# Stacking x1 on the hop-0 sums in a two-layer graph network: one product for x1 and its hop-1 share, own shares moved into the first row

## The chip, the core and the metric

The kernel runs on one core of a Trainium2 chip. The metric is device time in microseconds for one execution. The engines are called by short names: PE is TensorE (matmuls; PEld are its weight loads), DVE is VectorE, ACT is ScalarE, POOL is GpSimd, and SP issues the DMAs (SPq is its queue).

## What is computed

Two layers of a graph network over 4096 nodes with 64 features. The adjacency matrix `adj` is 4096 x 4096 fp32 and mostly zero. Layer 0 makes two hops, each with a sum over neighbours, a product with a weight matrix of 128 x 64 and a tanh. Layer 1 keeps, for each node, its last 100 neighbours at most, each weighted by a power of one half that depends on its rank in the row.

```python
# layer 0
h = maximum(layernorm(x), 0)
for k in range(2):
    agg = adj @ h
    h = tanh(concatenate([agg, h], axis=1) @ W[k])
x = x + h
# layer 1
h = maximum(layernorm(x), 0)
support = h @ weight
mask = (adj != 0)
rank = cumsum(mask, axis=1); deg = rank[:, -1:]
k = minimum(deg, 100); pos = rank - (deg - k)
w = mask * where(pos > 0, 0.5 ** (k - pos), 0)
x = x + (w @ support + bias)
```

## The kernel before

The nodes are cut into 4 chunks of 1024 (`NCH`, called `I`, or "rows" of the first sweep), each of 8 blocks of 128. Everything is fp32 but the layer-1 weights.

**Sweep 1** (lines 403 to 493) reads the whole matrix once, in 64 pairs of blocks `k` (16 pairs a row, so row 0 is pairs 0 to 15). `load` (line 411) issues the loads some pairs ahead, into a ring of three pair slots and into the areas that later hold the codes. For each pair two things happen. `count_pair` (line 232) marks the non-zero elements (on DVE at line 238, or before that on ACT by `mark_on_act`, lines 229 and 230, which for row 0 is written two pairs ahead) and counts them into codes, for layer 1. And TensorE adds `adj @ h` to the row's sums: at line 256 with 64 stationary columns into `acc_low` (two column halves `c` of the array side by side), or at line 468 ("fused") with 128 stationary columns, h0 and, for chunks whose x1 is already known, x1 as well, so that hop 1 is begun in the same pass. `features_T` (line 273, after pairs 4, 6, 9 and 13) transposes a chunk's h0 on TensorE into one of the two single-buffer PSUM banks `one` and `two` and ACT copies it into `pre1`, where it waits as the "own" operand.

At a row's end `finish_row` (line 338) is put on the list `steps`, of which each later pair runs one step. Step 1 copies the sums out of PSUM on ACT (`T` for h0's sums, `Fx` for x1's sums) and makes the row's totals (`totals`, line 286: an add on DVE, a cast on ACT). Step 2 is `x1_of` (line 213): two products, one with T and one with the own operand in `pre1`, into bank `po`, and a tanh on ACT (line 217) to `x1T`. Step 3 is `x1_and_share` (line 310): products of the transposed `Fx` with a weight (line 319) and of the transposed `x1T` with `both_w`, which is the identity beside the hop-1 weight (line 324). So the banks hold x1 by nodes and its share of hop 1; `take` (line 334) copies them out on ACT. Step 4 is `set_after` (line 291). In row 0 a further step adds the own-chunk sums.

**Sweep 2** (from line 764) reads the blocks of `adj` that hop 1 still lacks, 512 KB at a time, through the ring, and runs layer 1 at the same time. `finish_last` (line 503) finishes row 3 in steps, as `finish_row` does for the others. `finish_x2` (line 536) ends hop 1 of a chunk: S is copied from PSUM (line 541, ACT), four products `py` (line 551), add, tanh, residual, layernorm, and the features of layer 1. The order of all work is written out ahead by a planner in Python: `clock` holds a planned time for each engine, `use(engine, us, after)` moves it, and `decode`, `convert` (lines 637 to 663: code to weight, on ACT at 661 or DVE at 653 and 656), `settle` (line 396) and `layer1` (line 703) choose by these clocks what is written next. So a changed `use` can change the order.

The weights come in by one DMA, `load_weights` (line 147), issued before pair 9; POOL then spreads them (lines 151 and 154). POOL also has the `pow` of every layernorm (line 195).

Of the kernel before, what the change touches and what calls it, by code (L numbers as in the profile page):

```python
# [8 lines left out]
F32 = mybir.dt.float32  # L9
# [10 lines left out]
P = 128  # L20
# [23 lines left out]
def gnn_kernel(  # L44
# [73 lines left out]
    def tmp(shape=None, dtype=F32, name="tmp"):  # L118
        return tpool.tile(shape or [P, C], dtype, tag="tmp", name=name)
# [27 lines left out]
    def load_weights():  # L147
        nc.sync.dma_start(wb, weights)
        for h in range(2):
            rows = slice(h * D, (h + 1) * D)  # L150
            nc.gpsimd.tensor_copy(
                wz[rows, h], wb[rows, : HOPS * 2].rearrange("p (k a) e -> p k a e", a=2)
            )
        nc.gpsimd.tensor_copy(both_w[:, 1, :].rearrange("p (h e) -> p h e", h=2), wz[:, :, 1, 1, :])

    warm = spool.tile([P, 1], F32, tag="warm", name="warm")
    nc.vector.memset(warm, 0.0)
# [8 lines left out]
    both_w = cpool.tile([P, 2, P], F32, name="both_w")  # L166
    ident = both_w[:, 0, :]
    nc.vector.tensor_scalar(ident, diff, 0.0, None, op0=ALU.is_equal)

    tri = cpool.tile([P, P], BF16, name="tri")  # L170
    nc.vector.tensor_scalar(tri, diff, 0.0, -1.0, op0=ALU.is_lt, op1=ALU.mult)
# [32 lines left out]
    def paired(po, terms):  # L204

        for n, (w, v) in enumerate(terms):
            for c in range(NC):
                nc.tensor.matmul(  # L208
                    po[c * D : (c + 1) * D, :], w(c), v(c),
                    start=n == 0, stop=n == len(terms) - 1,  # L210
                )

    def x1_of(po, I, terms):

        paired(po, terms + [(lambda c: wz[:, c, 0, 1], lambda c: flat(pre1[:, chunk(I), :]))])
        x1T = tmp(name="x1T")
        nc.scalar.activation(x1T, po, AF.Tanh)
        return x1T

    as_nodes = lambda ap: ap.rearrange("p (c t) e -> p t c e", c=NC)  # L220

# [64 lines left out]
    def totals(I, both, tot):  # L286

        nc.vector.tensor_tensor(both.bitcast(U16), cnts[I % 2][0], cnts[I % 2][1], op=ALU.add)  # L288
        nc.scalar.copy(tot, both)  # L289
# [17 lines left out]
        )  # L307
        nc.vector.tensor_scalar(early, early, float(K), None, op0=ALU.min)

    def x1_and_share(I, x1T, Fx):  # L310

        banks = [one(name="pt"), two(name="pt")]
        v = by_t(x1T)
        for h, pt in enumerate(banks):
            pt = pt.rearrange("p (t w q) -> p t w q", t=2, w=2)
            if Fx is not None:
                f = by_t(Fx)
                for t in range(2):
                    nc.tensor.matmul(  # L319
                        pt[:, t, 1, :].rearrange("p (c e) -> p c e", c=NC), f[:, h, t, :], wz[:, :, 1, 0, :],  # L320
                        start=t == 0, stop=False, skip_group_check=True,
                    )
# [15 lines left out]
    def finish_row(I, acc, held):  # L338
        if I:

            T = [tmp(name="T") for _ in range(NC)]
            for c in range(NC):
                nc.scalar.copy(T[c][:D], acc[0][:D, c, :])
                nc.scalar.copy(T[c][D:], acc[1][c * D : (c + 1) * D])
# [4 lines left out]
        else:  # L349
            S = tmp(name="S")  # L350
            nc.scalar.copy(S, acc[1])
            Fx = None
# [50 lines left out]
    def sweep1():  # L403
# [28 lines left out]
        for k, (I, b) in enumerate(pairs):  # L432
# [3 lines left out]
            if k == 0:  # L436
# [66 lines left out]
    def finish_last(acc):  # L503

        I = NCH - 1
        bytes_ = mbuf.rearrange("p a r i -> p (a r i)")
        tot = bytes_[:, 2 * CW :].bitcast(BF16)
        totals(I, bytes_[:, :CW], tot)
        S = tmp(name="S")
        nc.scalar.copy(S, acc[1])  # L510
        F = [tmp(name="F") for _ in range(NC)]
        for c in range(NC):
            nc.scalar.copy(F[c], acc[0][:, c, :])
        Fx = tmp(name="Fx")
# [4 lines left out]
        po = one(name="po")  # L519
        x1T = x1_of(  # L520
            po, I, [(lambda c: wz[:, c, 0, 0], lambda c: S), (lambda c: wz[:, 0, 0, 0], lambda c: F[c])]
        )
        use("ACT", 0.65, use("PE", 2.3) + 0.2)
        yield
        banks = x1_and_share(I, x1T, Fx)
        take(hxs[I][:, :, D:], banks, 0)
        take(pre1[:, chunk(I), :], banks, 1)
        use("ACT", 1.5, use("PE", 2.8) + 0.2)
        yield
        set_after(I, tot, [one(name="pb"), two(name="pb")])  # L530
        feats[2] = place([P, CB, 2 * D], F32R, "cnt", "feat")
        use("DVE", 2.9, use("PE", 0.5) + 0.2)
        all_settle(I)
        space(feats[2].rearrange("p b d -> p (b d)"), clock["DVE"], 2)

    def finish_x2(I, acc):
# [1 line left out]

        h = chunk(I)
        S = tmp(name="S")  # L540
        nc.scalar.copy(S, acc)
        xres = tmp([P, CB, D], name="xres")
        nc.sync.dma_start(xres, x[I])
        state["gap"] = 1.35, 2.2
        t = use("ACT", 0.6, clock["PE"] + 0.2) + 0.1
        yield t

        pt = one(name="py")
# [364 lines left out]
```

## Time and profile before

| | |
|---|---|
| median of 3 runs | 368.76 us (367.73 to 369.48) |
| profiled execution, its own time | 367.51 us |
| its span in the profile | 365.7 us |
| PE busy | 340.6 us, 93% |
| DVE busy | 284.2 us, 78% |
| ACT busy | 205.3 us, 56% |
| POOL busy | 24.1 us, 7% |
| chain that ended last | PE 73%, DMA 15%, ACT 5%, SPq 4%, issue 2% |

The lines of the chain, by line of code, begin with PE L468 (23%), PE L256 into `acc` (16%), PE L703 (15%), PE L256 into `acc_low` (10%); the products that the change touches are L208 (3%), L319 (1%) and L324 (2%). The weights' DMA took 17.2 us from issue to landing.

How to read it: a row of a timeline has start, length, engine, line, operation, output and inputs, shape and count, and in brackets how long the engine stood idle before it and for whom. A matmul in fp32 has two records. The span leaves out some 1.8 us that the device time includes.

### The profile page before, as it was taken

The numbers are of one execution on the slowest core, as the hardware profiler recorded it, in microseconds if no ns is written. First come the engines' busy times: TensorE is split into PE (matmuls) and PEld (weight loads), VectorE is DVE, ScalarE is ACT, GpSimd is POOL, SyncE is SP. The second block draws the span as 40 slices with busy tenths as digits, with TensorE's granted clock in tenths as the row PEclk, the third lists the DMA queues.
The fourth block names the chain that finished last, engine by engine and source line by source line (L and its number), as shares of the span: only waits on it lengthen the run. The fifth ranks groups of instructions, "written<-read, shape, count | busy, mean of one in ns | idle before, by whom it ended". The sixth has DMA issues, their size and how long they took to land.

```text
span 365.7 us, 3966 instructions
## 1 busy us (share of the span) xinstructions
PE 340.6 (93%) x1356; PEld 151.9 (42%) x1356; DVE 284.2 (78%) x514; ACT 205.3 (56%) x230; POOL 24.1 (7%) x21
## 2 busy tenths in 40 slices
PE   3887789999999999999999998979999999989996
PEld 0242124333453444444444432333444444447585
DVE  4998989489998999979998965946587615858993
ACT  2286982576069260550000522777879699639991
POOL 2221100000000000000000002103100110003000
PEclk9999999999999999999999999999999999999998
DMA  7999999999994979639889989949888889830002
GB/s 289 414 409 407 408 409 409 409 411 407 409 398 185 356 283 392 237 117 359 324 299 340 314 270 411 323 169 323 311 286 284 318 293 318 328 126 0 2 30 86
DMA packets 29827, 108.45 MB, mean 297 GB/s; under 512 B 2416, under 2 KB 2800, under 8 KB 29808
## 3 DMA queue, kind: packets, MB, share of 16 engines
q1 hardware_dynamic: 29808, 108.21, 79.2%
q8 instruction: 10, 0.16, 0.2%
q14 instruction: 9, 0.07, 0.1%
HBM read 107.15 MB, written 1.05 MB: 296 GB/s over the span
## 4 chain that ended last, share of the span: by engine, by line
PE 73%; DMA 15%; ACT 5%; SPq 4%; issue 2%; DVE 0%; ACTq 0%
PE acc L468 23%; PE acc L256 16%; PE accl L703 15%; PE acc_low L256 10%; DMA codes<-in_adjA_dram 9%; DMA ring<-in_adjA_dram 6%; SPq L428 3%; PE po L208 3%; PE pto L754 2%; PE pt L324 2%; ACT weights L661 2%; PE py L551 1%; ACT codes L229 1%; PE pt L319 1%; ACT codes L230 1%
## 5 line engine op out<-in xcount | busy, mean ns | idle before, releaser
L661 ACT ACTIVATE weights<-codes,zero 128x1024 fp32r<-128x1024 uint8 x96 | 101.6, 1136 | 13.7 <-PE accl L703 10.4
L256 PE MATMUL acc<-ring,hx 128*64 128x512 f32 x288 | 70.9, 607 | 3.8 <-DMA ring<-in_adjA_dram 3.8
L703 PE MATMUL accl<-weights,feat 128*128 128x512 f32 x250 | 67.4, 409 | 0.7 <-ACT weights L661 0.6
L468 PE MATMUL acc<-ring,hx 128*128 128x512 f32 x152 | 66.1, 594 | 0.0
L256 PE MATMUL acc_low<-codes,hx 128*64 128x512 f32 x224 | 53.4, 599 | 6.4 <-DMA codes<-in_adjA_dram 6.4
L703 PEld LDWEIGHTS accl<-weights,feat 128*128 128x128 f32 x250 | 43.9, 188 | 31.0 <-ACT weights L661 15.0
L468 PEld LDWEIGHTS acc<-ring,hx 128*128 128x128 f32 x152 | 28.6, 190 | 37.1 <-issue 36.5
L250 DVE TENSOR_SCALAR cnt<-codes 128x512 uint16<-128x512 uint16 x128 | 37.7, 294 | 4.4
L249 DVE TENSOR_TENSOR codes<-mbuf,cnt 128x512 uint16<-128x512 uint16 x90 | 38.4, 426 | 3.1
L396 DVE TENSOR_TENSOR codes<-codes,after 128x2048 uint16<-128x2048 uint16 x32 | 37.7, 1218 | 0.0
L256 PEld LDWEIGHTS acc<-ring,hx 128*64 128x64 f32 x288 | 16.9, 135 | 43.9 <-issue 23.1
L256 PE MATMUL acc_low<-ring,hx 128*64 128x512 f32 x96 | 27.4, 692 | 7.7 <-DVE hx L198 6.3
L230 ACT ACTIVATE codes<-codes 128x1024 uint8<-128x1024 int8 x32 | 33.8, 1057 | 1.0
L238 DVE TENSOR_SCALAR mbuf<-ring 128x2048 uint8<-128x2048 f32 x27 | 32.9, 1220 | 0.8 <-DMA ring<-in_adjA_dram 0.8
L229 ACT ACTIVATE codes<-codes 128x1024 int8<-128x1024 f32 x24 | 25.1, 1047 | 11.7 <-DMA codes<-in_adjA_dram 11.7
L256 PEld LDWEIGHTS acc_low<-codes,hx 128*64 128x64 f32 x224 | 15.2, 136 | 37.8 <-issue 23.1
L656 DVE TENSOR_SCALAR weights<-bits 128x1024 fp32r<-128x1024 f32 x29 | 20.1, 694 | 9.9 <-PE accl L703 4.4
L238 DVE TENSOR_SCALAR mbuf<-codes 128x2048 uint8<-128x2048 f32 x21 | 25.6, 1219 | 0.0
L570 POOL TENSOR_TENSOR pre<-pre,wb 128x512 f32<-128x512 f32 x4 | 5.1, 1281 | 270.6 <-DVE xc L190 270.6
L289 ACT CAST mbuf<-mbuf 128x1024 bf16<-128x1024 uint8 x1 | 1.0, 1045 | 37.7 <-DVE mbuf L288 37.7
L653 DVE TENSOR_SCALAR bits<-codes 128x1024 uint32<-128x1024 uint8 x29 | 20.0, 690 | 0.6
L195 POOL TENSOR_TENSOR s<-s,half 128x8 f32<-128x8 f32 (+2 forms) x9 | 17.3, 1923 | 33.2 <-DVE s L194 33.2
(87 smaller groups left out, 252.3 us busy)
## 6 DMA issues: line engine op xcount, KB each, us to landing
ring<-in_adjA_dram SPq DMA_DIRECT2D x74, 512.0 KB, 4.8
codes<-in_adjA_dram SPq DMA_DIRECT2D x33, 1024.0 KB, 15.0
ring<-in_adjA_dram SPq DMA_DIRECT2D x30, 1024.0 KB, 5.6
pre<-in_x_dram SPq DMA_DIRECT2D x4, 256.0 KB, 6.9
xres<-in_x_dram SPq DMA_DIRECT2D x4, 256.0 KB, 5.8
out_dram<-o SPq DMA_DIRECT2D x3, 256.0 KB, 2.5
out_dram<-o SPq DMA_DIRECT2D x2, 128.0 KB, 2.0
wb<-in_weights_dram SPq DMA_DIRECT2D x1, 192.0 KB, 17.2
```

Source lines behind the costliest of these rows:

```text
L229: nc.scalar.activation(sign, a[:, r], AF.Sign)
L230: nc.scalar.activation(m, sign, AF.Square, scale=float((FLAG - 1 + 0.25) ** 0.5))
L238: nc.vector.tensor_scalar(m, a, 0.0, float(FLAG - 1), op0=ALU.not_equal, op1=ALU.mult)
L249: nc.vector.tensor_tensor(q, marks[r].bitcast(U16), cnt, op=ALU.add)
L250: nc.vector.tensor_scalar(cnt, q, 0x7F7F, None, op0=ALU.bitwise_and)
L256: nc.tensor.matmul(acc[c * D : (c + 1) * D, :], src, a[:, c * C : (c + 1) * C], start=first, stop=last,)
L396: nc.vector.tensor_tensor(q, q, a[:, None, :].to_broadcast([P, 4, CW // 2]), op=ALU.subtract)
L468: nc.tensor.matmul(acc[0][:, c, :], at(g), a[:, r, c * C : (c + 1) * C], start=g == CB * I - 1, stop=g == 0,)
L653: nc.vector.tensor_scalar(state["bits"], q, float(ZERO), ONE, op0=ALU.subtract, op1=ALU.mult)
L656: nc.vector.tensor_scalar(w, state["bits"].bitcast(F32), 2.0 ** (127 - LOW), None, op0=ALU.mult)
L661: nc.scalar.activation(w, q, AF.Exp, scale=LN2, bias=zero)
L703: nc.tensor.matmul(sums[g][:, c, :], feats[J][:, k, :], w[:, c * C : (c + 1) * C], start=first, stop=last,)
```

## The change

1. `load_weights` is issued before pair 6 instead of 9. `both_w` is split into `ident` and `xw`, whose rows 0 to 63 are the identity beside x1's hop-1 weight, and rows 64 to 127 zero beside the sums' hop-1 weight; POOL fills it with two copies.
2. x1 is no longer one tile with the two halves `c` above each other, but two tiles `xs[c]`: rows 0 to 63 get x1 of half c (one tanh for each), rows 64 to 127 get x1's sums (formerly `Fx`). One product of `xs[c]` with `xw` then gives x1 by nodes and the whole share. In row 0, which has no such sums, only 64 rows are used.
3. `own_share`: after pair 12 for chunk 2 and after pair 14 for chunk 1, the own product is made and copied back into `pre1`. In rows 1 and 2 `x1_of` leaves it out of the accumulation and adds it on DVE, into `T[1]`, before the tanh.
4. In `finish_row` the totals go from step 1 to step 2, behind x1.
5. `finish_last` stacks its sums as `finish_row` does (`T` from `acc` and `acc_low`), so that the three products of `x1_of` become two. Its `use` constants change.
6. In `finish_x2` the copy of S goes to ACT or DVE, whichever planned clock is behind.

```diff
-        nc.gpsimd.tensor_copy(both_w[:, 1, :].rearrange("p (h e) -> p h e", h=2), wz[:, :, 1, 1, :])
+        nc.gpsimd.tensor_copy(xw[:D, 1, :], wb[:D, 3, :])
+        nc.gpsimd.tensor_copy(xw[D:, 1, :], wb[D:, 2, :])
...
+    xw = cpool.tile([P, 2, D], F32, name="xw")
+    nc.vector.tensor_scalar(xw[:, 0, :], diff[:, :D], 0.0, None, op0=ALU.is_equal)
...
-    def x1_of(po, I, terms):
+    def x1_of(po, I, terms, xs, at_=None):
-        paired(po, terms + [(lambda c: wz[:, c, 0, 1], lambda c: flat(pre1[:, chunk(I), :]))])
-        x1T = tmp(name="x1T")
-        nc.scalar.activation(x1T, po, AF.Tanh)
-        return x1T
+        own = (lambda c: wz[:, c, 0, 1], lambda c: flat(pre1[:, chunk(I), :]))
+        paired(po, terms + [own] * (at_ is None))
+        if at_ is not None:
+            nc.vector.tensor_tensor(at_, po, flat(pre1[:, chunk(I), :]), op=ALU.add)
+            po = at_
+        for c in range(NC):
+            nc.scalar.activation(xs[c][:D], po[c * D : (c + 1) * D, :], AF.Tanh)
+
+    def own_share(I):
+        h = flat(pre1[:, chunk(I), :])
+        po = (two if I % 2 else one)(name="po")
+        paired(po, [(lambda c: wz[:, c, 0, 1], lambda c: h)])
+        nc.scalar.copy(h, po)
...
-    def x1_and_share(I, x1T, Fx):
+    def x1_and_share(I, xs):
         banks = [one(name="pt"), two(name="pt")]
-        v = by_t(x1T)
+        K_ = P if I else D
         for h, pt in enumerate(banks):
-            pt = pt.rearrange("p (t w q) -> p t w q", t=2, w=2)
-            if Fx is not None:
-                f = by_t(Fx)
-                for t in range(2):
+            pt = pt.rearrange("p (t w c e) -> p t w c e", t=2, w=2, c=NC)
+            for t in range(2):
+                for c in range(NC):
                     nc.tensor.matmul(
-                        pt[:, t, 1, :].rearrange("p (c e) -> p c e", c=NC), f[:, h, t, :], wz[:, :, 1, 0, :],
-                        start=t == 0, stop=False, skip_group_check=True,
+                        pt[:, t, :, c, :], by_t(xs[c])[:K_, h, t, :], xw[:K_],
+                        start=t == 0 and c == 0, stop=True, skip_group_check=True,
                     )
-            for t in range(2):
-                nc.tensor.matmul(
-                    pt[:, t, :, :], v[:, h, t, :], both_w,
-                    start=Fx is None and t == 0, stop=True, skip_group_check=True,
-                )
...
-            Fx = tmp(name="Fx")
+            xs = [tmp(name="x1T") for _ in range(NC)]
             for c in range(NC):
-                nc.scalar.copy(Fx[c * D : (c + 1) * D], acc[0][D:, c, :])
+                nc.scalar.copy(xs[c][D:], acc[0][D:, c, :])
...
-        tot = tmp([P, CW], BF16, name="tot")
-        totals(I, tmp([P, CW], U8, name="both"), tot)
+        both = tmp([P, CW], U8, name="both")
+        yield
+        x1_of(one(name="po"), I, terms, xs, T[1] if 0 < I < NCH - 1 else None)
+        tot = tmp([P, CW], BF16, name="tot")
+        totals(I, both, tot)
         yield
-        x1T = x1_of(one(name="po"), I, terms)
-        yield
-        banks = x1_and_share(I, x1T, Fx)
+        banks = x1_and_share(I, xs)
...
-            if k == 9:
+            if k == 6:
                 load_weights()
...
+            if k in (12, 14):
+                own_share({12: 2, 14: 1}[k])
...
-        S = tmp(name="S")
-        nc.scalar.copy(S, acc[1])
-        F = [tmp(name="F") for _ in range(NC)]
+        T, xs = ([tmp(name=n) for _ in range(NC)] for n in ("T", "x1T"))
         for c in range(NC):
-            nc.scalar.copy(F[c], acc[0][:, c, :])
-        Fx = tmp(name="Fx")
+            nc.scalar.copy(T[c][:D], acc[0][:D, c, :])
+            nc.scalar.copy(T[c][D:], acc[1][c * D : (c + 1) * D])
         for c in range(NC):
-            nc.scalar.copy(Fx[c * D : (c + 1) * D], acc[0][D:, c, :])
-        use("ACT", 2.8, 0.2)
+            nc.scalar.copy(xs[c][D:], acc[0][D:, c, :])
+        use("ACT", 3.4, 0.2)
...
-        use("ACT", 0.65, use("PE", 2.3) + 0.2)
+        x1_of(one(name="po"), I, [(lambda c: w0, lambda c: T[c])], xs)
+        use("ACT", 1.1, use("PE", 1.8) + 0.2)
...
-        use("ACT", 1.5, use("PE", 2.8) + 0.2)
+        use("ACT", 1.5, use("PE", 2.0) + 0.2)
...
-        nc.scalar.copy(S, acc)
+        if clock["ACT"] <= clock["DVE"]:
+            nc.scalar.copy(S, acc)
+            t = use("ACT", 0.6, clock["PE"] + 0.2) + 0.1
+        else:
+            nc.vector.tensor_copy(S, acc)
+            t = use("DVE", 0.7, clock["PE"] + 0.2) + 0.1
```

More of the change, by code (lines that the diff above doesn't have):

```diff
@@ L164, in gnn_kernel @@
     )
-    both_w = cpool.tile([P, 2, P], F32, name="both_w")
-    ident = both_w[:, 0, :]
+    ident = cpool.tile([P, P], F32, name="ident")
     nc.vector.tensor_scalar(ident, diff, 0.0, None, op0=ALU.is_equal)
+    xw = cpool.tile([P, 2, D], F32, name="xw")
+    nc.vector.tensor_scalar(xw[:, 0, :], diff[:, :D], 0.0, None, op0=ALU.is_equal)
     tri = cpool.tile([P, P], BF16, name="tri")
@@ L344, in finish_row @@
                 nc.scalar.copy(T[c][D:], acc[1][c * D : (c + 1) * D])
-            Fx = tmp(name="Fx")
+            xs = [tmp(name="x1T") for _ in range(NC)]
             for c in range(NC):
-                nc.scalar.copy(Fx[c * D : (c + 1) * D], acc[0][D:, c, :])
+                nc.scalar.copy(xs[c][D:], acc[0][D:, c, :])
             terms = [(lambda c: w0, lambda c: T[c])]
         else:
+            xs = [tmp(name="x1T") for _ in range(NC)]
             S = tmp(name="S")
             nc.scalar.copy(S, acc[1])
-            Fx = None
             terms = [(lambda c: wz[:, c, 0, 0], lambda c: S)]
+        both = tmp([P, CW], U8, name="both")
+        yield
+        x1_of(one(name="po"), I, terms, xs, T[1] if 0 < I < NCH - 1 else None)
         tot = tmp([P, CW], BF16, name="tot")
-        totals(I, tmp([P, CW], U8, name="both"), tot)
+        totals(I, both, tot)
         yield
-        x1T = x1_of(one(name="po"), I, terms)
-        yield
-        banks = x1_and_share(I, x1T, Fx)
+        banks = x1_and_share(I, xs)
         take(hxs[I][:, :, D:], banks, 0)
@@ L508, in finish_last @@
         totals(I, bytes_[:, :CW], tot)
-        S = tmp(name="S")
-        nc.scalar.copy(S, acc[1])
-        F = [tmp(name="F") for _ in range(NC)]
+        T, xs = ([tmp(name=n) for _ in range(NC)] for n in ("T", "x1T"))
         for c in range(NC):
-            nc.scalar.copy(F[c], acc[0][:, c, :])
-        Fx = tmp(name="Fx")
+            nc.scalar.copy(T[c][:D], acc[0][:D, c, :])
+            nc.scalar.copy(T[c][D:], acc[1][c * D : (c + 1) * D])
         for c in range(NC):
-            nc.scalar.copy(Fx[c * D : (c + 1) * D], acc[0][D:, c, :])
-        use("ACT", 2.8, 0.2)
+            nc.scalar.copy(xs[c][D:], acc[0][D:, c, :])
+        use("ACT", 3.4, 0.2)
         yield
[L519 to L522, printed above, removed]
-        use("ACT", 0.65, use("PE", 2.3) + 0.2)
+        x1_of(one(name="po"), I, [(lambda c: w0, lambda c: T[c])], xs)
+        use("ACT", 1.1, use("PE", 1.8) + 0.2)
         yield
-        banks = x1_and_share(I, x1T, Fx)
+        banks = x1_and_share(I, xs)
         take(hxs[I][:, :, D:], banks, 0)
         take(pre1[:, chunk(I), :], banks, 1)
-        use("ACT", 1.5, use("PE", 2.8) + 0.2)
+        use("ACT", 1.5, use("PE", 2.0) + 0.2)
         yield
@@ L544, in finish_x2 @@
         state["gap"] = 1.35, 2.2
-        t = use("ACT", 0.6, clock["PE"] + 0.2) + 0.1
         yield t
```

## The prediction

> **What bounds the kernel now.** I read the page first (TensorE busy 93% of the span, and 73% of the chain that ended last), then a table of windows, because a share over the whole span hides which stage an edit falls in. Columns: TensorE, its weight loads, VectorE, ScalarE, GpSimd busy (with counts), clock, DMA share, GB/s.
>
> ```profile
> 40.00:50.00 10.00, 7.61 (x46) 2.84 (x46) 9.08 (x21) 9.45 (x11) 1.23 (x3) 1.00 1.03 409
> 60.00:70.00 10.00, 10.00 (x48) 3.16 (x44) 7.77 (x16) 1.60 (x3) 0.00 (x0) 1.00 1.02 408
> 100.00:110.00 10.00, 10.00 (x47) 4.82 (x48) 9.38 (x20) 6.33 (x13) 0.00 (x0) 1.00 1.02 399
> 240.00:260.00 20.00, 17.38 (x73) 7.23 (x72) 13.59 (x19) 14.27 (x16) 3.84 (x2) 1.00 0.76 263
> ```
>
> Three regimes: until about 52 us the DMA paces the first row (409 GB/s, TensorE 7.6 of 10, ScalarE 9.45); from 54 to 213 us TensorE has no gap, so a microsecond added or removed there goes through; VectorE is just as full in row 1 and waits nowhere from 74 to 111 us. The second sweep (from 213) has holes. So the edits have to be placed. Timelines, first the end of row 0:
>
> ```profile
> 44.14 1.06 ACT L229 ACTIVATE codes<-codes 128x1024 int8<-128x1024 f32 x1
> 47.27 1.06 ACT L230 ACTIVATE codes<-codes 128x1024 uint8<-128x1024 int8 x1
> 48.23 0.61 ACT L282 COPY pre<-ph 128x512 f32<-128x512 f32 x1
> ...
> 45.93 1.04 PE L278 MATMUL ph<-both_w,hx 128*64 128x128 f32 x16
> 49.28 1.94 PE L256 MATMUL acc_low<-codes,hx 128*64 128x512 f32 x8 [0.59 <-DMA codes<-in_adjA_dram]
> 54.06 1.08 PE L208 MATMUL po<-S,wz 128*64 128x512 f32 x4 [0.28 <-ACT S L351]
> ```
>
> See that ScalarE copies the last feature transpose 1.3 us after TensorE made it, because four marking passes (44.14 to 48.3) stand before it. Row 1's finish:
>
> ```profile
> 101.98 0.58 ACT L344 COPY T<-acc_low 64x512 f32<-64x512 f32 x1
> 104.00 2.26 PE L256 MATMUL acc_low<-codes,hx 128*64 128x512 f32 x7
> 104.73 0.29 DVE L250 TENSOR_SCALAR cnt<-codes 128x512 uint16<-128x512 uint16 x1
> 104.85 0.60 ACT L217 ACTIVATE x1T<-po 128x512 f32<-128x512 f32 x1
> 106.19 0.74 PE L319 MATMUL pt<-wz,Fx 128*128 128x128 f32 x4
> 109.06 1.94 PE L256 MATMUL acc_low<-codes,hx 128*64 128x512 f32 x8
> ```
>
> VectorE ends the count of the pair after the row at 105.02; TensorE is ready for the share at 106.19. And chunk 2's second layer-0 hop:
>
> ```profile
> 239.20 1.19 PE L703 MATMUL accl<-weights,feat 128*128 128x512 f32 x4
> 242.34 1.21 PE L551 MATMUL py<-wz,S 128*128 128x128 f32 x8 [1.95 <-ACT S L541]
> ...
> 231.94 5.76 DVE L396 TENSOR_TENSOR codes<-codes,after 128x2048 uint16<-128x2048 uint16 x5
> 240.03 1.29 DVE L738 COPY parts<-accl 128x512 f32<-128x512 f32 x2 [2.33 <-PE accl L703]
> ...
> 240.69 1.13 ACT L661 ACTIVATE feat<-codes,zero 128x1024 fp32r<-128x1024 uint8 x1
> 241.72 0.56 ACT L541 COPY S<-acc 128x512 f32<-128x512 f32 x1
> ```
>
> TensorE stands 1.95 us for a ScalarE copy that is queued behind conversions, while VectorE is idle from 237.7 to 240.03.
>
> **What the Trainium skill says.** "TensorE: Matmul & The Clock Gate", on the array of 32×32 sub-arrays: ScalarE and VectorE are strict FIFO, and TensorE pulls only weight loads ahead. The copy at 48.23 agrees. The same page, "What's actually happening": an idle window of about 3.4 us halves the array clock. The trace has one such case: the first 8 matmuls take 3.68 us, later ones 1.94. "TensorEngine Tiling (Array Packing)", Key Properties: tiles of the array work independently. The trace agrees: at 101.85 the c=0 half of `po` runs on while c=1 waits for T. "VectorE: DVE Perf Modes", on PSUM operands: fp32 with a PSUM operand gets no faster mode. The L557 row (PSUM plus SBUF, 128x512) takes 0.69 us; I use that for the new add.
>
> **Part by part.** A matmul in fp32 is two records. A pair of column halves with 512 columns is 4 records in 0.86 us (L256: 32 in 6.89); a 128x128 product is 0.1175 us a record (L551: 8 in 0.94).
>
> *Start, weights.* One more small VectorE op at 1.4 us lies under a 1.83 us wait for x. The weight DMA goes three tiles earlier in SP's queue: wb lands after tile 9 (used at 32.76) plus 0.45 us of its own bytes, about 33.2, and tiles 10 to 12 come 0.45 later; the DMA has caught up by tile 13. GpSimd's copies (0.99, and two small ones, at most 0.29 each) now stand before chunk 0's `pow`, which started at 33.92: it starts near 34.6. VectorE's normalisation (35.70) slips 0.6 us, up to 1.5 if `pow` takes 2.6 as twice before. Cover: VectorE's 5.64 us wait at 73.82.
>
> *Own shares in row 0.* 4 records each after pairs 12 and 14. Their matmuls fit the DMA gaps, but chunk 2's uses the bank `one`, the pool has one buffer, and features_T(0) after pair 13 uses it again. It must wait for own_share(2)'s copy, which stands behind the four marks: 48.23 + 0.61 = 48.84, instead of running at 45.93. From there TensorE has no slack: transposes 0.87, pair 14 1.87, own_share(1) 0.86, pairs 15 and 16 3.74, so x1's product starts at 56.2 instead of 54.06: **+2.15**. ScalarE's extra copies end by 55.6, under this. Row 0's share is 16 records × 0.1175 = 1.88 against 1.93: nothing.
>
> *Row 1.* Removed: the own term, 0.86; share 2.87 (106.19 to 109.06) becomes 1.88. Added: VectorE's add between product and tanh, and a second tanh. The add stands behind the next pair's count: 105.02 − 0.34 (the totals add now comes after it) = 104.68; add to 105.39; the tanh halves (0.60 each, as the 64x512 T copies follow one another) to 106.0 and 106.6. TensorE would be free at 105.33. The share's second product waits until 106.65, then 14 records: 108.3 against 109.06: **−0.75**, where 1.85 was to be had. The pair that follows waits behind the share; so does nobody else.
>
> *Row 2.* VectorE, now with 0.71 more to do, reaches set_after only 0.2 us earlier than before. Same sum: count ends 150.77, add 151.5, second tanh 152.7, share ends 154.4 against 156.84: −2.4 in all, **−1.65** here.
>
> *Row 3.* VectorE's set_after: 157.35 against 159.14, so −1.8. Its mark of ring tile 51 frees the slot for tile 54 (issue 163.14, landing 4.8 later, needed 168.1). The tile comes 1.8 earlier, TensorE wants it 2.4 earlier, slack was 0.2: **+0.4**. In finish_last four T copies of 0.6 start only when acc is done (202.62), so c=1 starts at 205.1 instead of 204.3: 8 records end where 12 did; gain 0.06 instead of 0.86. Share again −0.99: **−1.05**. Net at 211.5 us: −0.9, and the ring loads of the second sweep wait for TensorE, so they move along.
>
> *Second sweep.* The planner chooses the engine of S by its own clocks. Followed with the constants of before, they stand at ACT 36.66, DVE 34.10 for chunk 2: S goes to VectorE; the changed constants move all clocks by about 1.3 alike. (Chunk 3: 15.20 to 16.65, stays; chunk 1: 74.36 to 74.51, a tie, and no wait hangs on it.) VectorE is free: S at 239.3 to 240.0, and py follows L703 at 240.4: **−1.95**. From 243 to 319 TensorE is nearly full, so it stays. Bounds: 0 if settles fill VectorE's gap (two more of 1.2), −2.4 with the 0.45 ScalarE gains.
>
> Sum: +2.15 −0.75 −1.65 +0.4 −1.05 −1.95 = **−2.85**. The profiled execution took 367.51 (span 365.70 and 1.81 around it), 1.25 below the median 368.76; carried to the median, **365.9**.
>
> **Rivals.**
> (B) The 1.95 us are not kept: S finds VectorE busy, or the re-planned order meets ring data (waits of 0.2 to 0.3 at 254 to 258) or a conversion. For: ScalarE is 91% busy from 260 to 280. Against: no TensorE wait over 0.3 us until 320. Then −0.9: 367.9.
> (C) The bank costs nothing, because the copy comes ahead of the marks. For: own_share's product is done by 44.1, just when the marks begin. Against: the marks of tile 13 are written at pair 11, and the queue is in order. Then −5.0: 363.8.
> (D) Slower: VectorE is one count further behind when x1's product is made. Each add then waits 2.66 us more, TensorE with it, in rows 1 and 2: −2.85 + 5.3 = +2.5: 371.2. It turns the sign once the count before the add ends 1.4 us later than reckoned, after 106.1. For: no VectorE wait from 74 to 111. Against: its 5.64 us wait at 73.82 ties it to TensorE.
> (E) The 2.9 us TensorE stand at 46 to 48.8 cools the array: one window at half speed, +1.7: 367.6. The skill's window is 3.4 us, so I give it little.
>
> **How the numbers follow.** Chances: forecast 0.54 (own range 364.7 to 367.1), B 0.23, C 0.10, D 0.08, E 0.05. A change of 0.5% (1.84 us) is about what a measurement tells from none. Below 366.9: most of the forecast's case (0.48), C, and a little of B: 0.62. Above 370.6: D and a bad order under B: 0.10. Same: 0.28. Range 364.1 to 369.0.
>
> **What would show it.** Right: features_T(0) starts near 48.8; the first row's x1 product near 56.2; in row 1 the share starts about 0.8 us after TensorE is free, waiting for ScalarE's tanh; S of chunk 2 on VectorE and no wait over 0.3 us before its py. Wrong: the transposes at 46, or a share wait of over 2 us, or the 1.95 us wait still there.

## The result: 1.95 us less in the medians, 0.7 us more in the two profiled executions

After: 367.50 us (median of 20 runs, 365.26 to 368.79), against 369.45 us for the kernel before on the same chip (20 runs, 367.44 to 371.72). The ratio is 0.994, with an interval of 0.9917 to 0.9963. The forecast was 365.9, range 364.1 to 369.0, and faster.

The profiled execution of after took 368.15 us (span 366.4), so it is 0.64 longer than the profiled one of before (367.51, span 365.7). The signs most likely differ because executions of one kernel differ by whether TensorE's clock falls to half somewhere: in the profiled execution of before it never does while TensorE has work, and in the one of after it does. So the trace is read stage by stage first. The stretches that answer to those shown of before (columns as there: TensorE, weight loads, VectorE, ScalarE, GpSimd, clock, DMA share, GB/s), and three that lie around the end of row 0:

```profile
40.00:50.00 10.00, 6.41 (x36) 2.80 (x34) 8.96 (x21) 8.59 (x10) 0.00 (x0) 0.91 1.03 410
60.00:70.00 10.00, 10.00 (x54) 4.45 (x52) 9.45 (x20) 1.88 (x4) 0.00 (x0) 1.00 0.95 363
100.00:110.00 10.00, 9.32 (x32) 3.41 (x31) 9.31 (x20) 4.87 (x9) 0.00 (x0) 1.00 0.99 385
240.00:260.00 20.00, 18.66 (x79) 8.12 (x79) 10.07 (x17) 15.71 (x18) 2.93 (x2) 1.00 0.83 286
...
46.00:48.80 2.80, 0.03 (x2) 0.04 (x2) 2.59 (x6) 2.68 (x4) 0.00 (x0) 0.89 1.03 410
48.80:51.00 2.20, 2.20 (x18) 1.97 (x20) 1.89 (x7) 0.21 (x1) 0.00 (x0) 0.50 1.02 410
51.00:53.00 2.00, 2.00 (x10) 0.66 (x8) 1.90 (x4) 1.97 (x3) 0.00 (x0) 0.85 1.04 416
```

Row 0 has more holes in TensorE than before (7.61 of 10 became 6.41), row 1 now has one (10.00 became 9.32); the second sweep has fewer (17.38 of 20 became 18.66); and the clock, which was 1.00 at 40 to 50 us, is at a half for over 2 us after the hole. In the next timelines the number in brackets is the time that the engine stood idle before the row; such an idle time is called a stand here. The timeline of after shows the hole of row 0:

```profile
46.11 1.04 ACT L242 ACTIVATE codes<-codes 128x1024 int8<-128x1024 f32 x1
47.18 1.06 ACT L243 ACTIVATE codes<-codes 128x1024 uint8<-128x1024 int8 x1
48.15 0.57 ACT L231 COPY pre<-po 128x512 f32<-128x512 f32 x1
48.77 1.98 PE L291 MATMUL ph<-ident,hx 128*64 128x128 f32 x16 [2.87 <-ACT pre L231]
50.53 2.43 PE L269 MATMUL acc_low<-codes,hx 128*64 128x512 f32 x8
57.08 1.03 PE L210 MATMUL po<-S,wz 128*64 128x512 f32 x4
```

The transposes wait 2.87 us for the copy of chunk 2's own share, which stands behind the marks; then they take 1.98 us where they took 1.04, and the pair after them 2.43 where it took 1.89. That is the half clock. The pair of before, which the forecast does not show:

```profile
46.80 1.89 PE L256 MATMUL acc_low<-codes,hx 128*64 128x512 f32 x8
```

Row 1's finish in after:

```profile
107.65 0.68 DVE L221 TENSOR_TENSOR T<-po,pre 128x512 f32<-128x512 f32 x1
108.37 1.28 ACT L224 ACTIVATE x1T<-T 64x512 f32<-64x512 f32 x2 [1.69 <-DVE T L221]
109.14 2.48 PE L332 MATMUL pt<-xw,x1T 128*128 128x128 f32 x16 [0.59 <-ACT x1T L224]
111.55 1.94 PE L269 MATMUL acc_low<-codes,hx 128*64 128x512 f32 x8
```

The share waits for the add and the tanh. Chunk 2's second hop, and what follows it, in after:

```profile
239.45 1.20 PE L713 MATMUL accl<-weights,feat 128*128 128x512 f32 x4
240.48 1.10 PE L561 MATMUL py<-wz,S 128*128 128x128 f32 x8
249.71 1.08 PE L269 MATMUL acc<-ring,hx 128*64 128x512 f32 x4 [0.21 <-DMA ring<-in_adjA_dram]
251.56 1.08 PE L269 MATMUL acc<-ring,hx 128*64 128x512 f32 x4 [0.77 <-DMA ring<-in_adjA_dram]
253.00 1.08 PE L269 MATMUL acc<-ring,hx 128*64 128x512 f32 x4 [0.36 <-DMA ring<-in_adjA_dram]
...
239.57 0.69 DVE L551 COPY S<-acc 128x512 f32<-128x512 f32 x1 [2.00 <-PE acc L269]
```

S is on VectorE and the 1.95 us wait is gone; 1.34 us of waits for ring tiles follow 9 us later, where before had 0.63 in three waits from 254 to 258. Last, the tail, first in before and then in after. The last row of conversions was 25 in 26.10 us and is now 26 in 27.13, and TensorE ran 64 records in 15.67 us without a halt where it now runs 50:

```profile
331.85 26.10 ACT L661 ACTIVATE weights<-codes,zero 128x1024 fp32r<-128x1024 uint8 x25
...
327.47 15.67 PE L703 MATMUL accl<-weights,feat 128*128 128x512 f32 x64
```

```profile
331.34 27.13 ACT L671 ACTIVATE weights<-codes,zero 128x1024 fp32r<-128x1024 uint8 x26
...
326.96 12.56 PE L713 MATMUL accl<-weights,feat 128*128 128x512 f32 x50
339.81 2.81 PE L713 MATMUL accl<-weights,feat 128*128 128x512 f32 x10 [0.29 <-ACT weights L671]
```

Starts on TensorE in the two profiled executions, and the gain or loss of each stage beside the forecast's term:

| TensorE starts | before | after | stage | forecast |
|---|---|---|---|---|
| x1 product, row 0 | 54.06 | 57.08 | +3.02 | +2.15 |
| pair after row 1's share | 109.06 | 111.55 | −0.53 | −0.75 |
| pair after row 2's share | 156.84 | 157.89 | −1.44 | −1.65 |
| first pair with the last finish | 202.51 | 203.67 | +0.11 | +0.4 |
| pair after row 3's share | 211.54 | 211.86 | −0.84 | −1.05 |
| py of chunk 2 | 242.34 | 240.48 | −2.18 | −1.95 |
| py of chunk 0 | 326.62 | 326.11 | +1.35 | 0 |
| end of the span | 365.7 | 366.4 | +1.21 | 0 |

### The profile page after: what moved, and what is told of

Its sections match the earlier page's. It is cut to its first block, busy times and chain, and to the rows that moved or that the text cites. A ratio compares the mean times of both kernels' runs of the same rounds, so it can differ in the third digit from the quotient of the medians.

```text
span 366.4 us, 3985 instructions
## 1 busy us (share of the span) xinstructions
PE 338.2 (92%) x1360; PEld 151.2 (41%) x1360; DVE 284.2 (78%) x515; ACT 209.6 (57%) x238; POOL 23.4 (6%) x22
## 3 DMA queue, kind: packets, MB, share of 16 engines
HBM read 107.15 MB, written 1.05 MB: 295 GB/s over the span
## 4 chain that ended last, share of the span: by engine, by line
PE 63%; DVE 13%; DMA 9%; ACT 8%; issue 4%; POOL 2%; DVEq 0%; POOLq 0%; ACTq 0%
PE acc L477 19%; PE acc L269 16%; PE accl L713 13%; DMA ring<-in_adjA_dram 8%; PE acc_low L269 7%; DVE codes L262 3%; DVE mbuf L251 3%; DVE cnt L263 3%; ACT codes L242 3%; PE pt L332 2%; ACT weights L671 2%; ACT codes L243 2%; PE pto L764 2%; PE po L210 2%; POOL s L197 2%
## 5 line engine op out<-in xcount | busy, mean ns | idle before, releaser
L269 PE MATMUL acc<-ring,hx 128*64 128x512 f32 x288 | 72.4, 608 | 4.6 <-DMA ring<-in_adjA_dram 4.6
L713 PEld LDWEIGHTS accl<-weights,feat 128*128 128x128 f32 x250 | 43.8, 188 | 32.3 <-ACT weights L671 17.6
L269 PE MATMUL acc_low<-ring,hx 128*64 128x512 f32 x96 | 25.1, 637 | 8.2 <-DVE hx L200 6.3
L742 DVE TENSOR_TENSOR parts<-accl,parts 128x512 f32<-128x512 f32 x16 | 10.3, 683 | 10.9 <-PE accl L713 10.9
```

Source lines behind the costliest of these rows:

```text
L269: nc.tensor.matmul(acc[c * D : (c + 1) * D, :], src, a[:, c * C : (c + 1) * C], start=first, stop=last,)
L713: nc.tensor.matmul(sums[g][:, c, :], feats[J][:, k, :], w[:, c * C : (c + 1) * C], start=first, stop=last,)
```

## Experiments

Each kernel has its own ratio to the kernel before, timed on the same chip: 368.22 us (40 runs) for the first four, 369.12 (43) for the next four, 368.69 (27) for the last three. Kernels of different groups are compared by these ratios; a ratio differs from the quotient of the two medians by up to 0.2%.

### The bank of row 0

`own_share` takes the bank `two` for both chunks, so that the transposes of chunk 0 find `one` free.

```diff
-        po = (two if I % 2 else one)(name="po")
+        po = two(name="po")
```

> The changed kernel, with both own shares in bank two, which is free at both places. Theory 1 (the bank holds TensorE until ScalarE has copied own_share(2), and the stand also cools the array): the 2.87 us wait before the last feature transposes goes, row 0's x1 product starts near 54.3 instead of 57.08, and the time is about 3.0 us below the changed kernel's, some 5 us below the kernel before (ratio near 0.987). Rival (the stand is hidden later, as row 0 is paced by the DMA): x1's product starts near 57 all the same, and the time stays within 0.5 us of the changed kernel's.

Measured: 364.59 us, ratio 0.9902 (0.9872 to 0.9931). The timeline of this kernel:

```profile
46.45 1.07 PE L291 MATMUL ph<-ident,hx 128*64 128x128 f32 x16
47.32 1.92 PE L269 MATMUL acc_low<-codes,hx 128*64 128x512 f32 x8
49.29 1.08 PE L210 MATMUL po<-pre,wz 128*64 128x512 f32 x4
54.90 1.08 PE L210 MATMUL po<-S,wz 128*64 128x512 f32 x4 [0.68 <-ACT S L360]
```

No wait ahead of the transposes, full clock (1.07 and 1.92), and x1's product at 54.90 instead of 57.08. So the wait was the single-buffer bank's, as the forecast put it, and one word takes it away: 0.38% between the ratios of this kernel and of after, 1.4 us, about half of the 3.0 that theory 1 had; their intervals just overlap, but the kernel that keeps the bank and was timed on the same chip (next) took 1.5 us longer too.

Next, the clock alone: the kernel after with three idle products in the hole.

```diff
+            if k == 13:
+                pw = two(name="pw")
+                for _ in range(3):
+                    nc.tensor.matmul(pw, ident, flat(pre1[:, chunk(1), :]), start=True, stop=True)
```

> The changed kernel with three idle products of 128x512 written into the stand (the wait for the bank stays, its result is not used), so that TensorE is busy for 2.6 of the 2.9 us. Theory 1 (part of the loss is the halved clock after the stand): the transposes and pair 14 run at full speed (1.04 and 1.9 us instead of 1.98 and 2.43), the time is about 0.9 us below the changed kernel's and varies less from run to run. Rival (the clock costs nothing net): the same time as the changed kernel within 0.3 us.

Measured: 366.10 us, ratio 0.9942 (0.9922 to 0.9962). In its profile the clock is 1.00 throughout 46 to 53 us, the transposes take 1.09 us, and x1's product starts at 56.05. From the transposes (49.12) to there it is 6.93 us, where after took 8.31 (48.77 to 57.08): 1.4 us was clock. The start is only 1.0 us earlier, as the idle products let the transposes begin 0.35 us later. The times don't show that microsecond: the ratio is that of after (0.994). What the idle products gain in the median is not resolved.

### Own shares at all

No `own_share`; the own product goes back into `x1_of` in every row, and the add on VectorE goes.

```diff
-        x1_of(one(name="po"), I, terms, xs, T[1] if 0 < I < NCH - 1 else None)
+        x1_of(one(name="po"), I, terms, xs)
...
-            if k in (12, 14):
-                own_share({12: 2, 14: 1}[k])
```

> The changed kernel without own shares: the own product is back in each row's x1 product, and no add on VectorE. Theory 1 (the own shares save nothing net, since the add on VectorE holds the share back as long as the product took): rows 1 and 2 gain 0.99 us each from the stacked share, against 0.68 and 1.44 measured, so the time equals that of the kernel with the other bank to within 0.3 us (ratio near 0.987). Rival (the own shares are what pays, 0.86 us a row): 1.7 us slower than with the other bank, near 0.991.

Measured: 364.30 us, ratio 0.9897 (0.9867 to 0.9926), the same as with own shares in a bank of their own. From x1's product of row 0 (54.07) to the pair after row 3's share (209.64) it needs 155.57 us; with own shares in bank `two` it is 155.04 (54.90 to 209.94). So they take 0.5 us off rows 1 and 2 and cost 0.8 in row 0, where that profile also has a 0.68 us wait for S. Row 1 tells why they bring so little: the own product took 0.86 us of TensorE, and the add and the tanh behind it take 0.59 back as a wait, in after and in the kernel with bank `two` alike.

### S of chunk 2

The kernel after with S always on ScalarE.

```diff
-        if clock["ACT"] <= clock["DVE"]:
+        if True:
```

> The changed kernel with S always copied on ScalarE, as before. Theory 1 (the copy on VectorE takes 1.8 us off chunk 2's wait, but half comes back as waits for ring data and one more conversion in ScalarE's tail): the 1.95 us wait before chunk 2's py returns, the waits of 0.77 and 0.36 us near 250 go, and the time is between 0.3 us below and 0.9 above the changed kernel's. Rival (the gain is kept to the end): 1.8 us slower than the changed kernel.

Measured: 369.88 us, ratio 1.0042 (1.0018 to 1.0066). The wait is back (1.94 us ahead of py), but the kernel lost more than either theory had: 1.02% against after, 3.8 us. Its profiled execution has three half-clock stretches, from 32.3, 49.4 and 244.0 us on, each of them 3.4 us long; the last begins 1.2 us after py. One such stretch takes 1.7 us, or 0.47% of the span, so a run whose mean clock is 0.995 or less has had at least one at work (behind the last product the profiles lose 1.2 us of clock at most). That holds for 18 of its 22 runs, and for 11 of the 20 of after. The wait and the stretch behind it:

```profile
242.76 1.21 PE L561 MATMUL py<-wz,S 128*128 128x128 f32 x8 [1.94 <-ACT S L548]
...
244.00:246.00 2.00, 2.00 (x6) 1.32 (x5) 1.99 (x3) 1.27 (x2) 0.00 (x0) 0.50 0.01 4
246.00:248.00 2.00, 2.00 (x8) 0.62 (x8) 1.81 (x3) 2.00 (x3) 0.04 (x1) 0.66 0.00 0
```

The rule by itself, in the kernel before:

```diff
-        nc.scalar.copy(S, acc)
+        if clock["ACT"] <= clock["DVE"]:
+            nc.scalar.copy(S, acc)
+            t = use("ACT", 0.6, clock["PE"] + 0.2) + 0.1
+        else:
+            nc.vector.tensor_copy(S, acc)
+            t = use("DVE", 0.7, clock["PE"] + 0.2) + 0.1
...
-        t = use("ACT", 0.6, clock["PE"] + 0.2) + 0.1
```

> The kernel before with the S rule alone (ScalarE or VectorE by the plan's clocks). The kernel before on the chip of the first runs: 368.22. Theory 1 (the rule is worth at its place the 1.95 us stand, plus what the array loses when that stand cools it in part of the executions, less about 0.9 given back at ring tiles near 250 us): 365.5 to 366.8, no TensorE wait over 0.3 us ahead of chunk 2's py, PE clock 1.00 from 240 to 250. Theory 2 (the re-planned order gives all of it back at ring tiles and in the tail): 368.0 to 368.5.

Measured: 364.62 us, ratio 0.9894 (0.9855 to 0.9933), better than theory 1 had. By the ratios this one part is worth more than the whole change (0.994), though the intervals overlap. Its profile has py at 239.59 instead of 242.34, and hardly a ring wait in the 60 us after it:

```profile
239.59 1.10 PE L555 MATMUL py<-wz,S 128*128 128x128 f32 x8
...
249.95 1.08 PE L256 MATMUL acc<-ring,hx 128*64 128x512 f32 x4 [0.16 <-DMA ring<-in_adjA_dram]
251.27 1.08 PE L256 MATMUL acc<-ring,hx 128*64 128x512 f32 x4 [0.24 <-DMA ring<-in_adjA_dram]
```

Its span is 2.3 us shorter than that of before (363.4 against 365.7); the medians differ by 4.5, the ratio makes it 3.9. All its six runs lie within 0.9 us and have a mean clock of 0.997 or more; those of before spread over 6.9 us, and 28 of 43 have a mean clock of 0.995 or less. So the rule does two things: it takes the wait, and it takes away a place where the clock can fall. The median of before is 1.25 us above that of its 15 runs without a fall (369.12 and 367.87), so by this estimate about one microsecond of the 4.5 is explained by neither. The counterpart, stacking alone (without own shares, S always on ScalarE):

```diff
-        if clock["ACT"] <= clock["DVE"]:
+        if True:
```

> The kernel after without own shares in the first row and with S always on ScalarE: the stacked share and the stacked sums alone. With the kernel before, with the rule alone and with both parts (364.3) it fills a table of two by two. Theory 1 (the parts add up, and S is worth in the medians the 3.7 us it was worth in the kernel after): 368.0, no change against the kernel before; the 2 us that TensorE is earlier at 211 us are lost in the stand ahead of chunk 2's py and in a half-clock stretch after it. Theory 2 (S is worth the bare 1.95 us of its stand, the stacking the rest): 366.2, with the stand of about 1.9 us but full clock after it.

Measured: 367.41 us, ratio 0.9956 (0.9932 to 0.998), between the two theories. TensorE is 2.7 us ahead of before at py of chunk 2 (239.62), and 0.15 us behind it at py of chunk 0 (326.77 against 326.62). Where it went is in the timeline and the windows of this kernel:

```profile
239.62 1.33 PE L559 MATMUL py<-wz,S 128*128 128x128 f32 x8 [1.92 <-ACT S L546]
240.60 2.05 PE L711 MATMUL accl<-weights,feat 128*128 128x512 f32 x4
253.00 1.08 PE L269 MATMUL acc<-ring,hx 128*64 128x512 f32 x4 [0.54 <-DMA ring<-in_adjA_dram]
255.93 1.08 PE L269 MATMUL acc<-ring,hx 128*64 128x512 f32 x4 [0.72 <-DMA ring<-in_adjA_dram]
```

```profile
239.00:241.00 2.00, 1.38 (x9) 1.39 (x10) 0.01 (x1) 0.56 (x2) 0.00 (x0) 0.89 0.47 178
241.00:243.00 2.00, 2.00 (x6) 1.40 (x5) 2.00 (x3) 1.29 (x2) 0.00 (x0) 0.50 0.02 4
243.00:245.00 2.00, 2.00 (x8) 0.57 (x8) 1.79 (x3) 2.00 (x3) 0.07 (x1) 0.76 0.00 0
```

The clock is the third column from the end: 0.89, 0.50, 0.76. The four records behind py took 2.05 us instead of 1.17 (the kernel without own shares that has S on VectorE). Summed over the three windows the clock lost 0.22 + 1.00 + 0.48 = 1.70 us. Up to py of chunk 0 the waits for ring tiles, two of which are shown, take 2.28 us, where before had 1.88, and S of chunk 1 is waited for another 0.55. That is 2.65 of the 2.87 us lost.

Does the stand bring the half clock? Two idle 128x512 products were put into it, in the kernel after with S on ScalarE, and then in the kernel before, which has no hole at the end of row 0:

```diff
         pt = one(name="py")
         v = by_t(S)
+        if I == 2:
+            for _ in range(2):
+                nc.tensor.matmul(pt, ident, flat(pre1[:, chunk(0), :]), start=True, stop=True)
```

> The kernel after with S always on ScalarE (369.88) and two idle 128x512 products (4 records, about 1.7 us) that TensorE makes while it waits for S of chunk 2. Theory 1 (the stand of 1.94 us lets the array's clock fall to half in part of the executions): PE clock 1.00 from 240 to 250, the pair after py 1.94 us instead of 2.41, and a median of 368.0 to 368.8. Theory 2 (the clock has nothing to do with the stand): a median of 369.7 to 370.1, low clock in 244 to 248 as before it.

Measured: 369.16 us, ratio 1.0021 (0.9998 to 1.0044), against 1.0042 without the products. In its profile the pair after py takes 1.94 us again, where it took 2.41. The median lies between the two theories, and 17 of its 22 runs still have a mean clock of 0.995 or less; row 0's hole is still in it. So this one does not tell.

> The kernel before with two idle 128x512 products (4 records, 1.88 us in an earlier run) in the 1.95 us in which TensorE waits for S of chunk 2; otherwise nothing is changed, so the transfer of work is the same and TensorE is about 0.3 us later. Theory 1 (that stand lets the array's clock fall in part of the executions, and this makes the medians of the kernel before and their spread): 366.3 to 367.4, most of the runs at a mean clock of 0.997 or more. Theory 2 (the stand has no part in the clock): the median of the kernel before or 0.3 us more, with the same spread.

Measured: 367.68 us, ratio 0.998 (0.9959 to 1.0001). 3 of 22 runs have a mean clock of 0.995 or less, against 12 of the 27 of before beside it, and one run of 22 is over 369 us, against 10 of 27. The two products are seen here, and py starts 0.1 us earlier than in before, as the stand was there anyway:

```profile
240.15 1.88 PE L552 MATMUL py<-pre,both_w 128*128 128x512 f32 x4
242.23 1.21 PE L554 MATMUL py<-wz,S 128*128 128x128 f32 x8 [0.20 <-ACT S L541]
```

The clock and the spread follow theory 1; the median lies 0.3 us above the range that it gave, and the interval just reaches 1. That the stand is a place where the clock falls is shown by the profiles and by the counts. Of the runs of before beside all experiments 59 of 110 have a mean clock of 0.995 or less; with the stand filled it is 3 of 22, and in the six kernels with S on VectorE and no hole in row 0 it is 2 of 36. It is not the only place: in the profiled execution of the kernel with idle products the clock falls at 31.8 us, after a stand of 2.12 us for a block of `adj` in row 0. In the three groups the median of before lies 0.44, 1.25 and 0.75 us above that of its runs without a fall; this is an estimate of what the falls put into it.

### The tail and the plan

One conversion more on VectorE ahead of chunk 0's last hop, in the kernel without own shares:

```diff
+        convert("DVE")
         layer1(2)
         convert("ACT")
         next(gen)
```

> The kernel without own shares (364.3), with one more conversion on VectorE just ahead of chunk 0's last hop, in the 4.1 us in which VectorE waits there. Theory 1 (the tail is paced by ScalarE's row of 26 conversions, so one fewer is worth one): 25 conversions after 327 us and 363.1 to 363.5. Theory 2 (the tail hangs on VectorE or TensorE as well): 364.0 to 364.6.

Measured: 363.62 us, ratio 0.9859 (0.9819 to 0.9899). 25 conversions remain, but from py of chunk 0 to the end it is 39.99 us, instead of the 40.33 without this edit (322.17 to 362.5): the conversion saved brings 0.3 us of its 1.04 in the profile, and the times don't tell it from 0.9897. Then the plan's three costs of the last row were put back to those of before, in the kernel without own shares, and nothing else:

```diff
-        use("ACT", 3.4, 0.2)
+        use("ACT", 2.8, 0.2)
...
-        use("ACT", 1.1, use("PE", 1.8) + 0.2)
+        use("ACT", 0.65, use("PE", 2.3) + 0.2)
...
-        use("ACT", 1.5, use("PE", 2.0) + 0.2)
+        use("ACT", 1.5, use("PE", 2.8) + 0.2)
```

> The kernel after without own shares (364.3 on another chip, span 362.5), with the plan's three costs of the last row put back to the values before, so that the second sweep is written in the order that the kernel before with the S rule has; nothing that is computed changes. Theory 1 (the new costs re-plan the order to one conversion more on ScalarE, and its row of conversions paces the tail): py of chunk 0 near 322.2, 39.0 to 39.3 us from there to the end instead of 40.3, a span of 361.2 to 361.6 and a median of 363.0 to 363.4. Theory 2 (the order has no part in it; a tail that starts earlier finds fewer conversions made): 39.9 or more from py to the end, a median of 364.0 to 364.6.

Measured: 363.51 us, ratio 0.9853 (0.9804 to 0.9902), span 360.9. The timeline of this kernel's tail, ScalarE and TensorE:

```profile
327.03 26.10 ACT L669 ACTIVATE weights<-codes,zero 128x1024 fp32r<-128x1024 uint8 x25
...
321.80 1.09 PE L559 MATMUL py<-wz,S 128*128 128x128 f32 x8
322.65 15.66 PE L711 MATMUL accl<-weights,feat 128*128 128x512 f32 x64
```

From py to the end 39.1 us instead of 40.3, and the run of 64 records of before is back. The profile shows theory 1; the ratios of the two kernels (0.9853 and 0.9897) have overlapping intervals. The new costs do it only together with the S rule: the two kernels that have them and S on ScalarE end with 25 conversions and 39.1 us. Both edits together:

> The kernel of the plan's old costs without own shares, and one conversion more on VectorE ahead of chunk 0's last hop. Theory 1 (both edits take from the same row of conversions on ScalarE, so they add up until TensorE paces the tail, in which it stood 0.9 us in the kernel before): 0.2 to 0.8 us under the run with the old costs alone, 362.4 to 363.0. Theory 2 (with the old costs TensorE paces the tail already): within 0.2 us of that run.

Measured: 362.47 us (360.41 to 365.12), ratio 0.982 (0.9769 to 0.9871), span 360.8: 24 conversions, 38.4 us from py to the end. It is the best of all, 6.2 us under before and 1.2% under after by the ratios; against the run with the old costs alone the intervals overlap, as its tail is 0.7 us shorter but its py comes 0.6 us later (322.41 instead of 321.80).

The parts in one table, as ratios to the kernel before:

| kernel | ratio | interval |
|---|---|---|
| S rule alone | 0.9894 | 0.9855 to 0.9933 |
| stacking alone, planned with the new costs | 0.9956 | 0.9932 to 0.998 |
| both, planned with the old costs | 0.9853 | 0.9804 to 0.9902 |
| both, planned with the new costs | 0.9897 | 0.9867 to 0.9926 |
| and own shares, in bank `two` | 0.9902 | 0.9872 to 0.9931 |
| and own shares, first one in bank `one` (after) | 0.994 | 0.9917 to 0.9963 |

The first two multiply to 0.9850, which agrees with the third (by the quotients of the medians it is 0.983 and 0.987). The new costs then add 0.44% (the profile has 1.2 us in the tail), own shares nothing, and the bank 0.38%. These last three steps are each within overlapping intervals; what shows them is the place in the profiles, not the ratio alone.

## Why the prediction was right in time and sign, and where its sum was off

**Row 0, +2.15.** Right in mechanism and place: transposes at 48.77 (48.84 was forecast), behind the copy behind the marks. The term was 0.9 us too small, because rival E happened on top of it: the hole halves the clock. That put 1.4 us on the way from the transposes to x1's product. Another 0.4 us went the other way: the forecast reckoned 1.87 us for each of three pairs, which take 1.72 once the clock is kept up, as its own price of 0.86 for half a pair would have given. So the 56.05 of the kernel with idle products, 0.15 from the forecast's 56.2, is near in part by luck. The forecast priced E's stretch rightly, at 1.7 us, but gave it 0.05, and this is the step that failed in it: "The skill's window is 3.4 us, so I give it little." A hole of 2.87 us was enough in the profiled execution of after. Eight of its 20 runs have a mean clock of 0.996 to 0.998 and lie at 365.3 to 366.3 us; the other twelve lie at 366.9 to 368.8, eleven of them at 0.995 or less.

**Rows 1 and 2, −0.75 and −1.65.** Right to 0.22 and 0.21 us: the share wait of 0.59 us for the tanh halves in row 1 was forecast as 0.8 after TensorE is free (the add began at 107.65, right behind a count). Rival D needed the count to end 1.4 us later; it didn't. In row 2 the add stands 0.40 us for TensorE, and no wait of the share is seen. That TensorE had no gap from 54 to 213 us was not quite so: it stood once, 0.3 us at 73, and nothing hangs on it.

**Row 3.** The stage with the ring tile cost 0.11 instead of 0.4, the finish gave 0.84 instead of 1.05. The 16 share records took 2.08 us from start to start (209.78 to 211.86), where 1.88 was reckoned from the records of py: 0.2 us, about what each of rows 1 to 3 fell short by.

**GpSimd's copies.** `pow` starts at 35.22, forecast near 34.6, and VectorE's normalisation 1.3 us later than before (36.97). TensorE doesn't feel it: in the kernel without own shares the transposes of chunk 0 start at 45.94, as before (45.93). Rival C fell with the transposes at 48.77.

**Second sweep, −1.95.** The wait went, S on VectorE, py right behind its predecessor: −2.18. The sentence that failed is "From 243 to 319 TensorE is nearly full, so it stays", with the one ahead of it, that the changed constants move all clocks alike. TensorE stood longer for ring tiles, 3.08 us up to py of chunk 0 where before stood 1.88, and of the 2.18 us 1.35 were gone there. This is not due to the plan: the kernel without own shares has the same one, stands 1.56 us, and takes as long from py of chunk 2 to py of chunk 0 as before (84.27 and 84.28). What sets when the tiles come stays open. And the plan made with the new costs and the S rule puts one conversion more on ScalarE in the tail, 1.21 us, which was no term of the sum at all. The run with the old costs shows that the costs do this and not the stacking. Rival B had both ("the re-planned order meets ring data" or "a conversion"); of the two only the conversion is shown to come from the order. B's 367.9 is nearer to the median than the forecast's 365.9.

**The base.** The forecast carried the profiled execution to the median by a constant of 1.25 us. That execution had no half-clock stretch at work after the start-up; about half of the runs of before (19 of 40 in the first group of experiments) have a mean clock of 0.995 or less, and their median there is 1.5 us higher (369.27 against 367.78). By moving S the change takes away a place where this happens, which no term of the sum contains, and with the bank it adds another. So the stage sum of the two profiles (+0.7) and the medians (−1.95) are both right, and that the forecast's −2.85 came near to the latter is partly luck, by errors of opposite sign: 2.6 us given back after 240 us that it did not see, and, most likely, a clock gain at the stand of the second sweep that it did not see either, 0.4 to 1.3 us in the median by the estimate above.

## What to carry to other kernels

When an edit borrows a single-buffer bank for work that is off the path, follow who takes the bank next and in which queue its release stands; here one line, another bank, was worth more than what the borrowed work brought. When an order is planned from costs, a corrected cost is itself an edit: plan with the old and the new costs, and time both. And where a kernel's runs spread by more than a per cent, look at the mean clock of each run before comparing a profile with a median: here a wait of 2 us on TensorE could cost nearly 4.

## What was not expected of the hardware

The half clock after short stands. "TensorE: Matmul & The Clock Gate", section "What's actually happening", has the clock fall after an idle window of about 3.4 us that runs freely. Here it fell after stands of 2.87 us (row 0 of after) and 1.92 us (stacking alone), so in these profiles a stand does not have to fill such a window, and the measurement decides.

The window itself is in the traces. Between the start-up and the last product the profiled executions have seven half-clock stretches: three in the kernel with S always on ScalarE, and one each in after, in stacking alone and in the two kernels with idle products at S. Each lasts 3.41 us and loses 1.70 or 1.71 us of clock; in after it is 0.31 + 1.10 + 0.30 in the three windows shown. The three of one execution begin at 32.33, 49.39 and 243.95 us, which is 5 and 57 times 3.413 us apart. So the clock falls and rises on a grid of 3.41 us, and each execution has its own phase of it. Where no fall at work gives the phase, the fall behind the last product does.

What counts is how much TensorE works within one stretch of the grid:

| kernel, and what it waits for | stretch of the grid, us | TensorE busy, us | clock of the next stretch |
|---|---|---|---|
| S always on ScalarE: the bank in row 0 | 45.97 to 49.39 | 0.78 | 0.50 |
| after: the bank in row 0 | 44.78 to 48.20 | 1.11 | 0.50 |
| before with idle products: a block of `adj` in row 0 | 28.42 to 31.83 | 1.34 | 0.50 |
| stacking alone: S | 237.15 to 240.56 | 1.49 | 0.50 |
| after with S on ScalarE and idle products: the bank | 45.04 to 48.46 | 1.46 | 1.00 |
| without own shares: a block of `adj` in row 0 | 27.19 to 30.61 | 1.69 | 1.00 |
| before: S | 240.86 to 244.28 | 1.94 | 1.00 |

In all thirteen profiles, from 14 us to the last product, there are eight stretches with at most 1.49 us of work. Seven of them were followed by the half clock, and no stretch with 1.69 us or more was. This is no bound for other work: behind the last products, which are small ones of 128x64, the clock fell after stretches with up to 2.65 us. This tells why the same stand of 1.9 us brings the half clock in some executions and not in others: with stacking alone it lay inside one stretch (237.7 to 239.62), and in before the grid cut it in two (240.39 to 242.34, cut at 240.86). It also tells why the fall can come after work has begun again. In after it came about 0.6 us before the transposes, with stacking alone about 0.9 us after the start of py, so nearly all of the half clock falls on the work behind the stand.
